# A mixture-of-experts layer with random-feature attention: the opening, the first expert and the closing blocks are put in another order, and the first expert's transposes are compared word by word

## The chip, the core and the metric

The kernel runs on one core of one Trainium2 chip. That core has five engines that run side by side, each on its own list of instructions: TensorE (PE in the profile) for matrix products and for transposes, VectorE (DVE), ScalarE (ACT), GpSimd (POOL), and SyncE (SP), which here only issues DMA transfers. Two sorts of DMA appear: SP's transfers go over one hardware queue, and the gathers and scatters with an index per row are issued by POOL on a software queue. The metric is the time on the device in microseconds (us), as the median of three runs.

## The reference

The input x has 4 x 2048 tokens of 512 numbers in fp32, 8192 tokens in all. Cut to what matters:

```python
xn  = layernorm(x)                                   # eps 1e-5
# attention by random features, 512 of them; ab = xis
def rfs(v): return exp(ab * (proj @ v) - 0.5 * |v|**2 * ab**2) * exp(ab) / sqrt(512)
attn = rfs(xn) @ rfs(input_weights).T                # input_weights: 512 x 512
# mixture of experts: 64 experts, 256 hidden units each
scores = sigmoid(xn @ router_w)                      # 8 groups of 8 experts
top 4 groups by their largest score, then the top 8 experts among them
w = chosen scores / their sum * 2.5
each expert takes its first 256 tokens, in the order of the tokens
e(t) = (silu(t @ gate_e) * (t @ up_e)) @ down_e
moe = sum over the chosen experts of w * e(xn)
      + (silu(xn @ sgate) * (xn @ sup)) @ sdown      # shared expert, for all tokens
out = x + attn + moe
```

## The kernel before

**Products.** Every fp32 matrix is split into a rounded part `hi` and a rest `lo`. `upper` (L96) makes `hi` as a copy on ACT, `rest` (L99) makes `lo` as a subtraction, on DVE unless told otherwise. `products` (L102, its matmul at L107) then sums three products, hi·hi, hi·lo and lo·hi. Transposes are done on PE against an identity matrix. A Tile scheduler puts each engine's instructions in order, following dependencies; `behind(a, b)` (L116) adds an ordering by hand: a is placed after b. Names with `_h` and `_l` in the profile are the two parts.

**Memory.** A pool of 40 slots of 4 KiB per partition (`kib4`, L83) holds almost everything: weights, tokens, transposed tokens, features. PSUM, where PE writes, is divided into three pools: `ps_tr` (2 banks), `ps_mm` (4) and `ps_sm` (2).

**Opening.** SP loads `ab`, the projection `pj`, the input weights `wi` (both in two transfers of 256 rows by `load_rows`, L142), the tokens of block 0, the router weights, and the shared expert's weights (`load_shared`, L167). `turn` (L293) transposes a matrix in 16 steps of 128x128 (`ps_x`) and splits the outcome; it is called for `pj` (`pT`), then for `wi` (`wT`), then for each block. `normalize(b)` (L254) takes mean and variance of each row by `bn_stats` on DVE, the reciprocal root by `inverse_root` (L223: a seed of two instructions on DVE, then three rounds of four small instructions on POOL), then `shift`, and last four ACT activations into `xw`. The row norms of tokens and weights go to a small DRAM array `norms` and come back, spread over all partitions, as `q` (`across`). `exponent` computes `ps_f`, the projections, and adds the norm term on DVE; its outcome for the weights is `fw`. `features_w` finishes the weights' features, `fW`.

**Blocks.** The tokens go in 16 blocks of 512 rows. `look_up(b)` (L311) is a generator: it transposes the normalised block (`xT`), computes the router's logits (`ps_l`, turned back by `ps_lt`), chooses experts on DVE, counts each expert's tokens into the DRAM array `upto`, and writes the normalised rows with their scores to `xnw`. `dense(b)` does the shared expert (`ps_gu`, then `ps_o` with `d_h`, `d_l`) and, for even blocks, the attention (`ps_f`, `fT`, `ps_o` with `fW`); its inner function `finish` (from L505) adds to the tokens and stores them in halves of 256 rows. Even blocks go through `dense` in the first 430 us. `routing(step)` between the steps drives the look-ups, one block per 5 steps. Odd blocks are only looked up; their transposes are kept in DRAM (`turned`), and their attention (`late_attention`: `ps_fu`, `ps_y`, copied to `yb` and stored to `attn`) fills the experts' loop.

**Experts.** `seek` (L674) is a generator that per step issues `find` for one expert, two indirect DMAs into `at` from `upto` (L651), and after every fourth expert runs `tokens_of` (L663 on), which compares `at` with the slot numbers on DVE and gives `who`, the token in each of the 256 slots. `gather(e)` (L700) issues two indirect DMAs that fetch an expert's rows, `xg`, from `xnw`. `turn_slots(e)` (L712) transposes them (`ps_t`), splits them into `gT`, and computes the weight `we` of each slot. At the end of the last even block the order is written by hand:

```python
for k in range(RC):
    for _ in range((2, 2, 1, 1)[k]):
        next(slots)
    next(rest_of)
for e in range(4):
    gather(e)
```

and three more steps of `slots` follow ahead of `turn_slots(0)`. The loop over experts (from L876) loads gate and up weights of expert i+2 and down weights of i+1, runs `hidden(i)` (`ps_gu`), takes a step of `slots`, gathers i+4, transposes i+1, and runs `down(i-1)` (`ps_e`), whose outcome is added to the output by an indirect DMA.

**Closing.** `ends` (L840) takes block 15 and the odd blocks 1, 3, ..., 13 through what is left of `dense`. `one(b)` fetches `xT_h` and `xT_l` from `turned` and, with `early`, the sums so far (`xo`, from the output) and `y` (from `attn`). It is called for the next block at step 2 of the block before, and two of the next block's steps are run at `left - 4` and `left - 2`.

## Time and profile before

| what | value |
|---|---|
| runs, us | 1354.17, 1352.31, 1350.28 (median 1352.31) |
| profiled execution, us | 1341.48 |
| its span, us | 1339.8 |
| mean granted PE clock | 0.994 |
| instructions | 21249 |
| DMA over the span | 327.07 MB, 244 GB/s |

The span is from the first to the last record of the profiled execution; its own time lies 1.7 us above. The chain that ended last is, by engine, PE for 64% of the span, DMA for 1%, and other engines for less than 1% each; by line, the experts' `ps_gu` has 34%, `ps_e` 13%, `ps_y` and `ps_fu` 5% each, `ps_o` 4% and `ps_t` 3%.

How the profile is read: a row such as `PE ps_x L301 <- ACT xw L278: 6.4, 5, 4.5` says that PE stood idle ahead of the instruction that writes `ps_x` at line 301, released by ACT's `xw` at line 278, 6.4 us in 5 waits, the longest 4.5. In a row of the timeline the first number is the start in us from the start of the span, the second the duration, then engine, line, operation, output<-inputs and their shapes, and in brackets the idle time ahead of it and its releaser. A row of forty digits shows tenths of busy time in equal slices of 33.5 us; PEclk is the clock that was granted to PE, in tenths of full speed.

### The profile page before, as it was taken

To read this page: it belongs to the slowest core of one execution; us is meant where nothing else is said; L and a number is where in the kernel's file an instruction comes from. 1 tells how busy PE (TensorE), PEld (TensorE's weight loads), DVE (VectorE), ACT (ScalarE), POOL (GpSimd) and SP (SyncE) were. 2 spreads that over 40 slices of the span, in tenths; PEclk is the share of its full clock that TensorE was granted. 3 is DMA by queue.
4 is the path that set the end of the run, shared out by engine and by line. 5 is a ranking of instruction groups with operands and counts; after the bars stand their busy time and mean duration, and the time that the engine had idled before them with its cause. 6 is when DMAs were issued, how large, how long until landed. Compare 5 with 4: busy or idle time off the path is not lost.

```text
span 1339.8 us, 21249 instructions
## 1 busy us (share of the span) xinstructions
PE 1311.0 (98%) x7648; PEld 1144.8 (85%) x7648; DVE 920.6 (69%) x1898; ACT 645.8 (48%) x1025; POOL 577.3 (43%) x684
## 2 busy tenths in 40 slices
PE   7899999999999899999999999999999999999998
PEld 6788888888888799999999999999999999978886
DVE  4887778768756477777677777777676777544455
ACT  5454434433433165556556655655564656531111
POOL 3321022022003575767776767767776755220000
PEclk9899999999999899999999999999999999999999
DMA  7465544554476799999999999999999989756996
GB/s 249 165 229 180 212 181 158 212 208 155 172 261 211 237 252 279 294 273 247 306 269 287 279 284 278 259 288 278 269 279 293 279 239 282 206 141 236 311 314 207
DMA packets 186266, 327.07 MB, mean 244 GB/s; under 512 B 15536, under 2 KB 87216, under 8 KB 186160
## 3 DMA queue, kind: packets, MB, share of 16 engines
q1 hardware_dynamic: 153392, 245.93, 53.5%
q0 software_dynamic: 32768, 79.78, 26.7%
q8 instruction: 60, 0.98, 0.3%
q14 instruction: 46, 0.38, 0.1%
HBM read 220.66 MB, written 104.99 MB: 243 GB/s over the span
## 4 chain that ended last, share of the span: by engine, by line
PE 64%; DMA 1%; DVE 0%; ACT 0%; issue 0%; DVEq 0%
PE ps_gu L107 34%; PE ps_e L107 13%; PE ps_y L107 5%; PE ps_fu L107 5%; PE ps_o L107 4%; PE ps_t L721 3%; DMA xT_l<-turned 1%; DMA at<-upto,line 0%; PE ps_f L107 0%; DVE f L454 0%; DVE d_l L100 0%; DVE at L663 0%; ACT f L467 0%; DVE xo L508 0%; ACT fT L97 0%
## 5 line engine op out<-in xcount | busy, mean ns | idle before, releaser
L107 PE MATMUL ps_gu<-gT,gu_h 128*128 128x256 f32 x2048 | 294.3, 284 | 0.0
L771 POOL DMA_INDIRECT out_dram<-ye,who x128 | 221.1, 1727 | 143.7 <-DMA out_dram<-ye,who 57.0
L107 PEld LDWEIGHTS ps_gu<-gT,gu_h 128*128 128x128 f32 x2048 | 269.6, 192 | 7.3 <-ACT gu_h L97 0.5
L651 POOL DMA_INDIRECT at<-upto,line x128 | 148.1, 1157 | 82.3 <-DVE first_of L645 43.6
L704 POOL DMA_INDIRECT xg<-xnw,who x128 | 136.7, 1068 | 88.7 <-issue 62.6
L107 PE MATMUL ps_gu<-gT,gu_l 128*128 128x256 f32 x1024 | 166.7, 285 | 0.0
L100 DVE TENSOR_TENSOR gu_l<-gu,gu_h 128x1024 fp32r<-128x1024 f32 x128 | 155.9, 1220 | 4.9 <-ACT gu_h L97 4.1
L107 PE MATMUL ps_e<-d_h,ehT 128*128 128x512 f32 x512 | 148.7, 392 | 0.0
L107 PEld LDWEIGHTS ps_gu<-gT,gu_l 128*128 128x128 f32 x1024 | 140.7, 191 | 1.2
L97 ACT CAST gu_h<-gu 128x1024 fp32r<-128x1024 f32 x128 | 132.2, 1059 | 0.0
L230 POOL TENSOR_TENSOR a<-rstd,ve 128x4 f32<-128x4 f32 x48 | 10.9, 227 | 265.5 <-DVE rstd L228 262.9
L97 ACT CAST ehT<-sg 128x512 fp32r<-128x512 f32 x64 | 39.8, 621 | 172.4 <-DVE sg L462 172.4
L107 PEld LDWEIGHTS ps_e<-d_h,ehT 128*128 128x128 f32 x512 | 94.6, 188 | 18.8
L770 ACT ACTIVATE ye<-ps_e,we 128x512 f32<-128x512 f32 x128 | 88.5, 698 | 37.0 <-PE ps_e L107 37.0
L462 DVE SCALAR_TENSOR_TENSOR sg<-sg,ps_gu 128x512 f32<-128x512 f32 x64 | 44.0, 688 | 78.7 <-PE ps_gu L107 78.5
L100 DVE TENSOR_TENSOR d_l<-d,d_h 128x1024 fp32r<-128x1024 f32 x64 | 78.3, 1223 | 10.1 <-ACT d_h L97 10.0
L460 ACT ACTIVATE sg<-ps_gu 128x512 f32<-128x512 f32 x64 | 38.4, 600 | 95.8 <-PE ps_gu L107 95.8
L100 DVE TENSOR_TENSOR gT<-ps_t,gT 128x512 fp32r<-128x512 f32 x128 | 83.3, 683 | 0.2 <-ACT gT L97 0.2
L107 PE MATMUL ps_e<-d_l,ehT 128*128 128x512 f32 x256 | 79.2, 390 | 1.0 <-DVE d_l L100 1.0
L107 PE MATMUL ps_o<-fW_h,fT 128*128 128x512 f32 x288 | 79.7, 391 | 0.3 <-ACT fT L97 0.2
L107 PE MATMUL ps_o<-d_h,hT 128*128 128x512 f32 x256 | 79.8, 399 | 0.0
L461 DVE SCALAR_TENSOR_TENSOR sg<-sg,ps_gu 128x512 f32<-128x512 f32 x64 | 43.9, 685 | 43.5 <-ACT sg L460 43.4
(173 smaller groups left out, 2544.4 us busy)
## 6 DMA issues: line engine op xcount, KB each, us to landing
gu<-in_L_ffn_gate_w_dram SPq DMA_DIRECT2D x64, 512.0 KB
gu<-in_L_ffn_up_w_dram SPq DMA_DIRECT2D x64, 512.0 KB
d<-in_L_ffn_down_w_dram SPq DMA_DIRECT2D x64, 512.0 KB
xnw<-xw SPq DMA_DIRECT2D x32, 577.0 KB
xb<-in_L_attn_x_dram SPq DMA_DIRECT2D x32, 512.0 KB
out_dram<-xb SPq DMA_DIRECT2D x32, 512.0 KB
xT_h<-turned SPq DMA_DIRECT2D x30, 512.0 KB
xT_l<-turned SPq DMA_DIRECT2D x30, 512.0 KB
```

The costliest lines, as they stand in the source:

```text
L97: return nc.scalar.copy(dst, src)
L100: return on.tensor_tensor(dst, src, hi.bitcast(FP), ALU.subtract)
L107: last["pe"] = nc.tensor.matmul(ps, w[c][a], v[c][b], start=(start and part == 0 and c == 0), stop=(stop and part == 2 and c == n - 1),)
L230: nc.gpsimd.tensor_tensor(a, y, v, ALU.mult)
L460: nc.scalar.activation(dst, g, AF.Tanh, scale=0.5)
L461: nc.vector.scalar_tensor_tensor(dst, dst, 1.0, g, ALU.add, ALU.mult)
L462: nc.vector.scalar_tensor_tensor(dst, dst, 0.5, u, ALU.mult, ALU.mult)
L651: nc.gpsimd.indirect_dma_start(out=at[:, e % TE, h, :], out_offset=None, in_=upto, in_offset=bass.IndirectOffsetOnAxis(ap=line[:, e, h : h ...
L704: nc.gpsimd.indirect_dma_start(out=xgs[e][:, h, :], out_offset=None, in_=xnw, in_offset=bass.IndirectOffsetOnAxis(ap=who[:, e, h : h + 1], ...
L721: turned_s = nc.tensor.transpose(ps_[:, c, ts(h, P)], xr[:, h, ts(c2 * 2 + c, P)], ident_r)
L770: nc.scalar.activation(ye[:, h, :], po, AF.Copy, scale=wes[e][:, h : h + 1])
L771: now = nc.gpsimd.indirect_dma_start(out=out, out_offset=bass.IndirectOffsetOnAxis(ap=who[:, e, h : h + 1], axis=0), in_=ye[:, h, :], in_o ...
```

## The change

In the opening, `wi` is loaded first and in four pieces of 128 rows, then `ab`, `pj`, block 0, the router weights, block 1, and the shared weights. The weights' norms come from `bn_stats` of `wi` in place of four squares on ACT. `wi` is transposed ahead of `pj`. `normalize` is divided in three: `statistics`, `roots`, and what is left. Block 0's root runs on DVE throughout (the others stay on POOL), and block 1's statistics and root are ordered ahead of block 0's transposes. The projections of the weights (`projected`) take the banks of `ps_sm` and `ps_tr`, block 0's transposes those of `ps_mm`; the four additions into `fw` come behind block 0's split. The rests of the shared weights (`gu_l`, `d_l`) move from POOL to DVE. `normalize(1)` comes ahead of block 0's logits, and `look_up(1)` starts one step later.

At the experts, two steps of `slots` are taken in each of the four places ahead of the gathers (eight in place of six), and two in place of three afterwards. For expert 0 `turn_slots` transposes the rows a second time, in fp32, into another bank (`p32`); ACT copies it out, DVE compares it with the first transposes word by word and counts the equal words. The weights `we` of expert 0 are multiplied by 1 if all are equal, and by a large other number if not.

In the closing, the copies into `yb` are placed behind the split of the last down weights once that is issued; `xT` and `y` of the next block are fetched at the start of a block, ahead of `xo`; the first of the two early steps moves one step up for block 15; `finish`'s addition of `y` is placed behind the last DVE instruction noted; and block 13, stored last, is stored in quarters of 128 rows.

```diff
-    def load_rows(src, name):
+    def load_rows(src, name, at_once=2):
...
-            nc.sync.dma_start(t, src[ts(k, 2 * P), :].rearrange("(s p) d -> p s d", p=P))
+            for s in range(0, 2, at_once):
+                r0 = (2 * k + s) * P
+                nc.sync.dma_start(
+                    t[:, s : s + at_once, :],
+                    src[r0 : r0 + at_once * P, :].rearrange("(s p) d -> p s d", p=P),
...
     last = {}
+    late_blocks = range(1, NB - 1, 2)
+    last_stored = late_blocks[-1]
+    wi = load_rows(iw, "wi", 1)
     ab = const.tile([P, RC], FP, name="ab")
     nc.sync.dma_start(ab, xis.rearrange("(c p) -> p c", p=P))
     pj = load_rows(proj, "pj")
-    wi = load_rows(iw, "wi")
     xbs = {0: load_tokens(0)}
...
-    def load_shared():
+    def load_shared_gates():
...
+    def load_shared_down():
...
-    sgu, sd = load_shared()
...
+    xbs[1] = load_tokens(1)
+    sgu = load_shared_gates()
+    sd = load_shared_down()
...
-    def inverse_root(y, v):
...
+    def statistics(rows_of, after=NS * [None]):
...
         for s in range(NS):
+            last["stats"] = nc.vector.bn_stats(st, rows_of[s])
+            if after[s] is not None:
+                behind(last["stats"], after[s])
...
+    def roots(b, mv, on=nc.gpsimd):
...
+        inverse_root(rstd, ve, on)
...
+        on.tensor_tensor(shift, mv[:, :, 0], rstd, ALU.mult)
+        last["shift"] = on.tensor_scalar(shift, shift, -1.0, None, ALU.mult)
...
+    def normalize(b, rstd, shift):
...
-            ((ps_tr, "tr"), (ps_sm, "sm")),
+            ((ps_tr, "tr"), (ps_sm, "sm")) if b else ((ps_mm, "mm"),),
...
+    def projected(v, rc, ps):
         products(ps, parts(pT, KC, ts(rc, P)), v, True, True)
...
+    def exponent(dst, nsq, rc, ps):
...
-                nc.vector.tensor_tensor(xb[s], xb[s], y[s], ALU.add)
+                behind(nc.vector.tensor_tensor(xb[s], xb[s], y[s], ALU.add), last["dve"])
             last["dve"] = nc.vector.tensor_tensor(xb[s], po, xb[s], ALU.add)
             done.append(s)
-            if s ^ 1 in done:
-                k = s // 2
-                store_rows(b, k, xb)
+            if b == last_stored:
+                r0 = b * TB + s * P
+                nc.sync.dma_start(out[r0 : r0 + P, :], xb[s])
+            elif s ^ 1 in done:
+                store_rows(b, s // 2, xb)
...
                 last["dve"] = nc.vector.tensor_copy(yb[:, s % 2, :], po)
+                if "down" in last:
+                    behind(last["dve"], last["down"])
...
+    wmv = statistics(wi)
+    wT = turn(lambda s: wi[s], "wT", ((ps_tr, "tr"), (ps_sm, "sm")))
+    wq = const.tile([P, NS], FP, name="wq")
+    nc.gpsimd.tensor_tensor(wq, wmv[:, :, 0], wmv[:, :, 0], ALU.mult)
+    nc.gpsimd.tensor_tensor(wq, wq, wmv[:, :, 1], ALU.add)
+    nc.gpsimd.tensor_scalar(padded[2][:, :NS], wq, -0.5 * H, None, ALU.mult)
+    as_row(NB, padded[2])
+    wn = across(NB)
     pT = turn(lambda s: pj[s], "pT", ((ps_mm, "mm"),))
-    wT = turn(lambda s: wi[s], "wT", ((ps_tr, "tr"), (ps_sm, "sm")))
...
     normed = {}
-    normed[0] = normalize(0)
-    first, root = last["stats"], last["root"]
-    wq = const.tile([P, NS], FP, name="wq")
-    for s in range(NS):
-        sq = act.tile([P, H], FP, tag="t", name="sq")
-        squared = nc.scalar.activation(sq, wi[s], AF.Square, accum_out=wq[:, s : s + 1])
...
-    def split_gates(gu, on=nc.vector, after=None):
-        hi = [kib4([P, KC, I], "gu_h") for _ in range(2)]
...
-            if after is not None:
-                behind(a, after[0])
...
+    normed[0] = normalize(0, *roots(0, statistics(xbs[0], NS * [last["rest"]]), nc.vector))
+    first = last["shift"]
+    roots1 = roots(1, statistics(xbs[1], NS * [first]))
+    seed1 = last["seed"]
+    def split(t, name, after=(None, None)):
+        hi, lo = kib4(list(t.shape), name + "_h"), kib4(list(t.shape), name + "_l")
+        both = upper(hi, t), rest(lo, t, hi)
+        last["split"] = both[1]
+        for a, b in zip(both, after):
...
-    shared_gu = split_gates(sgu, nc.gpsimd, (squared, root))
...
+    sgate = split(sgu[0], "gu", (None, seed1))
+    ps_w = []
+    for rc in range(RC):
+        pool, tag = ((ps_sm, "sm"), (ps_tr, "tr"))[rc // 2]
+        ps_w.append(pool.tile([P, H], FP, tag=tag, name="ps_f"))
+        projected(parts(wT, KC), rc, ps_w[rc])
+    late = look_up(0)
+    next(late)
+    upper0 = last["upper"]
+    sup = split(sgu[1], "gu", (upper0, last["rest"]))
     fw = Chunks(RC, "fw", FP)
     for rc in range(RC):
-        ps = ps_mm.tile([P, H], FP, tag="mm", name="ps_f")
-        exponent(fw[rc], parts(wT, KC), wn, rc, ps)
+        exponents = exponent(fw[rc], wn, rc, ps_w[rc])
+        behind(exponents, last["rest"])
+    normed[1] = normalize(1, *roots1)
+    shared_w = list(zip(sgate, sup)), split(sd, "d", (upper0, exponents))
...
-    xbs[1] = load_tokens(1)
-    late = look_up(0)
-    next(late)
-    normed[1] = normalize(1)
     next(late)
     next(late)
-    shared_w = shared_gu, split_down(sd, nc.gpsimd)
...
-        nc.scalar.activation(f, f, AF.Exp, scale=ab[:, rc : rc + 1])
+        behind(nc.scalar.activation(f, f, AF.Exp, scale=ab[:, rc : rc + 1]), upper0)
         behind(nc.vector.tensor_scalar(f, f, coef[:, rc : rc + 1], None, ALU.mult), first)
...
+        if e == 0:
+            same = rt.tile([P, KC // 2], FP, tag="same", name="same")
...
+            if e == 0:
+                p32 = ps_mm.tile([P, 2, CAP], FP, tag="mm", name="ps_t32")
+                for c in range(2):
+                    for h in range(NH):
+                        nc.tensor.transpose(
+                            p32[:, c, ts(h, P)], xg[:, h, ts(c2 * 2 + c, P)], ident
+                        )
+                like = act.tile([P, 2, CAP], FP, tag="t", name="like")
+                nc.scalar.copy(like, p32)
+                nc.vector.tensor_tensor(like, like, ps, ALU.is_equal)
+                nc.vector.tensor_reduce(same[:, c2 : c2 + 1], like, AX.XY, ALU.add)
...
         )
         behind(shares, turned_r)
         nc.vector.reciprocal(we, we)
+        if e == 0:
+            for c2 in range(KC // 2):
+                k = same[:, c2 : c2 + 1]
+                nc.vector.tensor_scalar(k, k, -float(2 * CAP), 1.0e6, ALU.add, ALU.mult)
+                nc.vector.tensor_scalar(k, k, 1.0, None, ALU.add)
+                nc.vector.tensor_scalar(we, we, k, None, ALU.mult)
         wes[e] = we
...
+        if k == (b == 1) and b < NB:
             fronts[b] = look_up(b)
...
-            normed[b + 1] = normalize(b + 1)
+            normed[b + 1] = normalize(b + 1, *roots(b + 1, statistics(xbs[b + 1])))
...
                 if n == 8:
                     for k in range(RC):
-                        for _ in range((2, 2, 1, 1)[k]):
+                        for _ in range(2):
                             next(slots)
                         next(rest_of)
...
-        if n < 3:
+        if n < 2:
             next(slots)
...
+        def one(b, w, xT, y, early):
...
-                y = load_rows(attn[ts(b // 2, TB), :], "y") if b in late_blocks else None
                 return load_rows(out[ts(b, TB), :], "xo"), y
-            xT = fetch_block(b)
...
+        cur, left = one(order[0], w, fetch_block(order[0]), None, False)
...
+            if n + 1 < len(order):
+                b = order[n + 1]
+                fetched = fetch_block(b), load_rows(attn[ts(b // 2, TB), :], "y")
+            whole = n == 0
...
-                    nxt, steps = one(order[n + 1], w, True)
-                if nxt is not None and k in (left - 4, left - 2):
+                    nxt, steps = one(b, w, *fetched, True)
+                if nxt is not None and k in (left - 4 - whole, left - 2):
                     next(nxt)
...
             dws[i] = split_down(downs.pop(i))
+            if i == E - 2:
+                last["down"] = last["split"]
```

## The prediction, made before the changed kernel ran

> **What bounds the kernel now.** I read the page first: shares of the engines, then the 40 slices.
>
> ```profile
> PE 1311.0 (98%) x7648; PEld 1144.8 (85%) x7648; DVE 920.6 (69%) x1898; ACT 645.8 (48%) x1025; POOL 577.3 (43%) x684
> ...
> PE   7899999999999899999999999999999999999998
> ...
> DVE  4887778768756477777677777777676777544455
> ...
> PEclk9899999999999899999999999999999999999999
> ```
>
> TensorE is the bound and is almost never idle. All that a change of order can win lies in span minus PE busy, 1339.8 - 1311.0 = 28.8 us, plus the time in which PE ran at a lower granted clock. Digits below 9 stand at the start, in slice 14 (about 450 us) and at the very end. DVE is near 9 in slices 2 and 3: there a second engine is nearly full. Next the view of waits for PE over the whole span:
>
> ```profile
> PE ps_x L301 <- ACT xw L278: 6.4, 5, 4.5
> PE ps_x L301 <- DMA pj<-_L_attn_proj_matrix_dram: 6.0, 2, 5.3
> PE ps_t L721 <- DVE gT L100: 5.9, 1, 5.9
> PE ps_gu L107 <- DMA xT_h<-turned: 1.8, 2, 1.3
> ...
> PE ps_e L107 <- DVE d_l L100: 1.0, 1, 1.0
> ```
>
> (us in total, times, longest; a sixth line, for xT_l, has 0.5.) Five places hold nearly all of the idle time. The stretches of PE alone show what follows an idle gap (us, PE busy, clock, DMA share, GB/s):
>
> ```profile
> 40.00:42.00 2.00, 0.26 (x2) 1.00 0.94 354
> ...
> 44.00:45.00 1.00, 0.25 (x1) 0.50 0.00 0
> ...
> 49.00:50.00 1.00, 1.00 (x6) 0.50 0.00 0
> ...
> 460.00:462.00 2.00, 0.28 (x2) 0.50 0.48 172
> ```
>
> A gap of 4 us or more is paid twice: idle, then about 5 us at half clock. Last, the timeline at these places:
>
> ```profile
> 26.10 2.72 DVE L454 SCALAR_TENSOR_TENSOR fw<-q,ab,ps_f 128x512 f32<-128x512 f32 x4 [8.38 <-DMA q<-norms]
> ...
> 115.06 1.91 PE L301 MATMUL ps_x<-ident,xw 128*128 128x128 f32 x16
> 116.73 0.71 PE L107 MATMUL ps_o<-d_h,hT 128*128 128x512 f32 x2
> ...
> 444.42 0.79 PE L721 MATMUL ps_t<-ident_r,xg 128*128 128x128 f32 x8
> ...
> 459.84 1.23 DVE L663 TENSOR_TENSOR at<-at,slot 128x1024 f32<-128x1024 f32 x1 [5.98 <-DMA at<-upto,line]
> ...
> 1196.00 0.90 SPq L145 DMA_DIRECT2D xo<-out_dram  x2
> ...
> 1197.00 0.89 SPq L532 DMA_DIRECT2D xT_h<-turned  x2
> ...
> 1335.89 0.37 SPq L154 DMA_DIRECT2D out_dram<-xo  x1
> ```
>
> **The change part by part.** Pitches (start to start) at full clock from the timeline: a 128x512 product 0.228 us, 128x256 0.115, an fp32 transpose 0.104 (115.06 to 116.73, 16 of them).
>
> *Opening, up to the first ps_f of block 0 (52.56 us before).* The weight rows come first and in four pieces. Before, the first 1.05 MB had landed at 6.62, so wi is in by about 6.0, pj by 9 at the 370 to 400 GB/s of those stretches. 12 + 16 transposes at the cold 0.21 (16 in 3.35 us) end at 12.2 (before 12.7). 48 ps_f follow: 10.95, to 23.2. Meanwhile DVE ends pT_l at 13.6, takes four bn_stats (2.8, as at 14.29 to 17.06) and then the root itself: 17 dependent small steps of 0.18 (17.19, 17.35, 17.55), to 19.5. On POOL these steps are 0.28 apart and a gu_l of 2.4 us stood between them: shift came at 23.94. ACT needs 2.93 for the four xw: 22.4, ahead of PE's 23.2. So block 0's 16 transposes follow without a gap and at full clock: 1.7, to 24.9, where before they ended at 29.90. xT_h costs 0.4; then 48 ps_gu, 8 ps_l, 4 ps_lt (13.2) and block 1's transposes (1.7): 40.2. Block 1's statistics and roots are now ahead of all of it, and gu_l and d_l are off POOL, so the 4.5 us wait goes.
>
> ACT loses the four squares and their sums (0.8 each). SP gets two more issues (0.5 each) for wi and block 1's load ahead of sgu; sgu is first needed at 16, so that costs nothing. Late next is q: its norms rows are queued on SP behind sgu and sd, so q is issued at about 23.5, and q took 5.3 (20.84 to 26.10): 29. ps_l now needs a PSUM bank that ps_f holds until fw has read it: 30.2 against PE's 29.2, 1.0 lost: 41.2, a lead of 11.4. This is not kept. Onto DVE come two gu_l (2.4), d_l (1.2) and the root (2.5). In the new order about 30.5 us of DVE work stand between fw and block 0's last feature; from 29.4 that is 59.9, and its rounded copy 61.2, then four xw of block 2 to 64.2. PE would be there at 59 and be through block 2's first transposes and 23 ps_o at 64.3, where before it stood at 72.4. The lead left is 8; I take 7.8. look_up(1) one step later is in that order. From 100 on DVE is at 75% or less and PE waits 2 us in 350: nothing more to win, and cover for the rest.
>
> *Expert 0 (450 to 467).* DVE stood 5.98 us behind a gather of `at` before it could split gT; PE lost 5.9 idle and then 2.1 (its work of 461.7 to 466.8 needs 3.0 at full clock, took 5.1): 8.0. Now finds 4 to 7 are issued ahead of the four token gathers and this `at` is read before expert 0 is turned. Price: POOL issues four more finds (1.25 each) first, of which 3.9 fall into its idle time before 434.7; gather 0 is 1.1 later, its second half lands at 437.1 + 6.6 = 443.7, PE needs it at 444.2. The last find lands at about 435 + 6.5 = 441.5, DVE is there at 440: 1.5 lost, bounds 0 and 4.3 (landings 3.5 to 9.3).
>
> The fp32 check: 8 transposes x 0.104 = 0.83 on PE. On ACT two copies (0.6 each), on DVE two compares (0.69), two reduces (0.6) and six small steps (0.17): 3.6 us of DVE. Expert 0's 48 products (5.5 us) hide them, and the weights `we` are needed only by down(0), a round later; but the second half of gT and the next PSUM bank wait behind the first compare: 0.5. Without the cover all 3.6 would count. No compare of this form is in the trace; gT's split, PSUM and SBUF in 0.68, is the nearest row. Part: 8.0 - 1.5 - 0.83 - 0.5 = 5.2.
>
> *Here a rule speaks against the change.* Row: 16 transposes at 115.06 run in 1.67 us, and the clock in 115 to 121 stays 1.00. The Trainium skill (TensorE: Matmul & The Clock Gate, Part 4: PE-mode transpose) says that transposes do not count as PE work for the clock; Part 1 gives windows of 3.4 us. By the rule block 0's and block 1's transposes, now behind each other's products, could each leave 3.4 us at half clock, 1.7 twice: 3.4 less. By the row it is nothing. The row is this kernel's own; 3.4 goes into the range.
>
> *Last expert.* PE waited 1.0 for d_l behind a yb copy; the copy is now held back behind d_l (1.22); behind it on DVE and SP stand only ehT and attn's store, which no one needs for 20 us: 1.0. *First late block.* xT was queued on SP behind xo, which waits for the last scatter; now xT and y go first: 1.8 + 0.5 = 2.3. Its cover is DMA: 0.94 busy at 1240 to 1320, so y and xT earlier use slices 34 and 35 (206 and 141 GB/s). *Last store.* From issue to end 3.9 us for 512 KB; a quarter-block of 256 KB at 330 GB/s saves 0.8, less an issue: 0.7 (bounds 0 and 1).
>
> Sum 7.8 + 5.2 + 1.0 + 2.3 + 0.7 = 17.0. The profiled execution took 1341.48 (span 1339.8), so 1324.5. The median of the runs, 1352.31, is 0.8% above it; no view says why. I scale: 17.1, 1335.2.
>
> **Rivals.**
> *DVE takes the opening (chance 0.2).* For it: DVE 8 or 9 tenths in slices 2 and 3, and 6.1 us more work. Against: before, PE waited there only 0.2. If half of the 7.8 goes, or the clock rule holds: 13 to 14 less than before, 1338.5 to 1339; with both, 10.
> *The wait at expert 0 only moves (0.1).* If find or gather lands 3 to 5 us later, PE idles before ps_t and the half clock returns: the part is 0, 12 less, 1340.
> *Slower (0.05).* SP is one queue. The new buffer order shifts which of the 40 slots each weight load waits for; if gates of an expert come late for ACT's cast in the 62 rounds of the loop, each costs PE. Against: between 500 and 1160 ACT waits for no load, and PE is 100% busy. A lateness beyond the slack by 0.28 us per round eats the 17.1; 0.4 us gives -17.1 + 24.8: 1360. It decides from a load some 4 us later than now.
> *The gains do not come about (0.05),* as when the opening is bound by loads and the clock anyway: 1350 to 1354.
>
> **How the numbers follow.** Likeliest (0.6): 1335.2, own range 1330 to 1340, from DVE giving back 1 to 6, `at` 0 to 4.3, store 0 to 1. The range to hold 8 in 10 takes in the first two rivals and, below, 7 us of which the opening's full lead makes 3.6: 1328 to 1345. A measurement can tell 0.3%, 4 us. Faster 0.90, same 0.05, slower 0.05.
>
> **What would show it.** Right: the waits of PE lose ps_x on xw, ps_t on gT, ps_e on d_l and ps_gu on xT; clock 1.00 from 13 us on; first ps_f of block 0 near 41; PE idle about 15 in all, half of it start and end. Half wrong: PE waiting at 29 to 33 on fw or at 60 to 65 on fT or xw; ps_t waiting on xg or on DVE's `at` or compare near 435 to 445. Wrong: ACT gu_h waiting for DMA in the loop, clock 0.50 after a run of transposes, or DMA waits of ps_gu after 1215.

## The result, and the profile after

| | runs | median, us | ratio to before |
|---|---|---|---|
| before | 4 | 1351.30 (1349.63 to 1354.17) | |
| after | 4 | 1337.38 (1335.18 to 1338.81) | 0.9892 (95% interval 0.9871 to 0.9913) |

The changed kernel is 13.9 us faster; 17.1 was forecast, and 1335.2 us against 1337.4 measured. That the two figures lie so close is in part luck, as the traces show. One thing must be known to read any number below: the kernel before takes about 1341 us in one series of runs and about 1351 in three others, among them these; its profile of 1341.48 us belongs to the first sort, the changed kernel's profile (1338.81 us, span 1337.1) to the second. The two profiles can therefore not simply be subtracted. The three series of experiments below ran on three different chips: number 15 where before has 1341, numbers 14 and 2 where it has 1351. For the runs of the table the chip is not known. Whether the chip makes the difference was not tested.

The page of the changed kernel, the lines that answer to those of before:

```profile
PE 1310.4 (98%) x7656; PEld 1146.4 (86%) x7656; DVE 930.8 (70%) x1932; ACT 646.7 (48%) x1019; POOL 569.1 (43%) x670
...
PE   8999999999998899999999999999999999999998
...
DVE  7978768767764577777777767667776776653555
...
PEclk9999999999998899999999999999999999999999
```

PE's busy time is as it was; DVE has 10 us more. The start has gained (8, 9, 9 where 7, 8, 9 stood, and the clock's first digit below 9 is gone), but slices 13 and 14, about 400 to 470 us, are now both at 8. The waits of PE in the changed kernel (us in total, times, longest):

```profile
PE ps_y L107 <- ACT fU L97: 5.7, 1, 5.7
PE ps_x L323 <- DMA wi<-_attn_input_weights_dram: 5.4, 3, 4.0
PE ps_gu L107 <- issue: 4.5, 8, 1.4
PE ps_lt L368 <- ACT lt L361: 2.2, 1, 2.2
```

All four waits that the prediction wanted gone are gone: for xw, for gT, for d_l and for xT. Three have come: for lt in the opening, for fU at 431 us, and eight ahead of expert 0's products at 445 to 458 us that no engine releases. The timeline of the changed kernel shows the second and third:

```profile
429.19 0.75 DVE L478 SCALAR_TENSOR_TENSOR f<-q,ab,ps_fu 128x512 f32<-128x512 f32 x1 [4.49 <-remote]
...
431.39 0.79 PE L107 MATMUL ps_y<-fW_h,fU 128*128 128x512 f32 x1 [5.75 <-ACT fU L97]
...
446.64 1.33 PE L107 MATMUL ps_gu<-gT,gu_h 128*128 128x256 f32 x9 [1.40 <-issue]
...
453.15 0.36 PE L107 MATMUL ps_gu<-gT,gu_l 128*128 128x256 f32 x1 [1.03 <-issue]
```

DVE stands 4.49 us ahead of an addition whose only open input is ps_fu, and PE's last product into ps_fu had ended at 420.9, 8 us earlier. Everything after it (fU, then ps_y) is late by that. After each of the two places PE runs at half clock for 6.8 us (from 427.8 and from 455.1). Idle PE and work lost to half clock (taken as half of PE's busy time in it) come to 15.2 us between 420 and 480 us, where the profile of before has 8.3.

The most useful view for the whole question is the lead: the start of a PE product in the kernel before, less the start of the same product in the other kernel, read from the two timelines. A column's time is that of the kernel before. The row of the result stands against the first profile of before, all others against its second, taken in the series where before has 1341 us ("before again", span 1340.8).

| kernel (series by before's median) | first ps_f of block 0 | 100 us | 434 us | 783 us | block 15, 1190 us | block 1, 1225 us | last product | span |
|---|---|---|---|---|---|---|---|---|
| prediction | 11.4 | 7.8 | 7.8 | 13.0 | 14.0 | 16.3 | 16.3 | 17.0 |
| after, result (1351) | 7.9 | 8.1 | 8.7 | -0.8 | 0.3 | 3.5 | 3.9 | 2.7 |
| after again (1341) | 10.3 | 10.4 | 11.0 | 15.2 | 16.5 | 21.8 | 22.5 | 21.2 |
| no compare (1341) | 8.6 | 8.7 | 9.3 | 9.9 | 10.9 | 16.2 | 16.9 | 15.6 |
| free y (1341) | 8.5 | 8.6 | 9.2 | 14.0 | 15.2 | 20.5 | 20.6 | 20.8 |
| opening only (1351) | 9.1 | 8.9 | 9.5 | 3.0 | 0.7 | -0.3 | 0.1 | 0.2 |
| slots undone (1351) | 8.8 | 9.0 | 9.6 | -2.7 | -2.1 | 3.2 | 4.0 | 3.0 |
| lt first (1351) | 12.5 | 12.6 | 13.6 | 2.8 | 4.0 | 9.3 | 10.0 | 8.7 |
| after third (1351) | 10.6 | 10.0 | 10.5 | 4.0 | 5.2 | 10.5 | 11.2 | 10.0 |
| three mends (1351) | 13.5 | 13.6 | 14.5 | 6.9 | 7.3 | 12.7 | 13.2 | 13.3 |
| closing undone (1351) | 8.3 | 8.4 | 8.9 | 0.4 | 0.2 | 0.8 | 1.0 | 0.7 |
| at later (1351) | 9.5 | 9.6 | 9.6 | -0.9 | 0.4 | 5.7 | 6.5 | 5.2 |
| compare eight (1351) | 9.0 | 9.2 | 9.9 | -23.3 | -22.1 | -16.8 | -16.0 | -16.9 |

Between 434 and 783 us every row from a series of 1351 loses 6 to 13 us (the last one 33, of which more below); in the other series two of three gain there and one stands still.

### The profile page after: what moved, and what is told of

It is laid out like the page before. It is cut to its first block, busy times and chain, and to the rows that moved or that the text cites. A ratio compares the mean times of both kernels' runs of the same rounds, so it can differ in the third digit from the quotient of the medians.

```text
span 1337.1 us, 21310 instructions
## 1 busy us (share of the span) xinstructions
PE 1310.4 (98%) x7656; PEld 1146.4 (86%) x7656; DVE 930.8 (70%) x1932; ACT 646.7 (48%) x1019; POOL 569.1 (43%) x670
## 4 chain that ended last, share of the span: by engine, by line
PE 94%; DVE 2%; ACT 1%; issue 1%; DMA 1%; POOL 0%; another core or an unknown queue 0%; SPq 0%; ACTq 0%; DVEq 0%
PE ps_gu L107 41%; PE ps_o L107 14%; PE ps_e L107 13%; PE ps_f L107 6%; PE ps_y L107 6%; PE ps_fu L107 6%; PE ps_t L757 3%; PE ps_l L351 2%; PE ps_x L323 2%; DMA pj<-_L_attn_proj_matrix_dram 1%; PE ps_lt L368 1%; DVE r L486 0%; DVE st L274 0%; DVE f L478 0%
## 5 line engine op out<-in xcount | busy, mean ns | idle before, releaser
L826 POOL DMA_INDIRECT out_dram<-ye,who x128 | 226.2, 1767 | 190.5 <-ACT ye L825 127.1
L685 POOL DMA_INDIRECT at<-upto,line x128 | 139.7, 1092 | 82.2 <-DVE first_of L679 43.5
L245 POOL TENSOR_TENSOR a<-rstd,ve 128x4 f32<-128x4 f32 x45 | 11.2, 249 | 270.6 <-DVE rstd L241 268.3
L486 DVE SCALAR_TENSOR_TENSOR sg<-sg,ps_gu 128x512 f32<-128x512 f32 x64 | 44.0, 687 | 67.6 <-PE ps_gu L107 54.6
L492 ACT ACTIVATE f<-f,ab 128x512 f32<-128x512 f32 x64 | 46.2, 722 | 77.3 <-DVE f L478 63.2
L100 DVE TENSOR_TENSOR gT<-ps_t,gT 128x512 fp32r<-128x512 f32 x128 | 83.2, 682 | 0.1
L100 DVE TENSOR_TENSOR ehT<-sg,ehT 128x512 fp32r<-128x512 f32 x64 | 44.3, 692 | 51.4 <-ACT ehT L97 43.8
```

The lines of the kernel that those rows point to most:

```text
L100: return on.tensor_tensor(dst, src, hi.bitcast(FP), ALU.subtract)
L486: nc.vector.scalar_tensor_tensor(dst, dst, 0.5, u, ALU.mult, ALU.mult)
L492: nc.scalar.activation(f, f, AF.Exp, scale=ab[:, rc : rc + 1])
L685: nc.gpsimd.indirect_dma_start(out=at[:, e % TE, h, :], out_offset=None, in_=upto, in_offset=bass.IndirectOffsetOnAxis(ap=line[:, e, h : h ...
L826: now = nc.gpsimd.indirect_dma_start(out=out, out_offset=bass.IndirectOffsetOnAxis(ap=who[:, e, h : h + 1], axis=0), in_=ye[:, h, :], in_o ...
```

## The experiments

### Series 1: both kernels again, without the compare, and with y free

**before_again** and **after_again**: no edit.

> The kernel before, unchanged, to see whether the profiled execution of 1341.48 us, 9 to 13 us under its timed runs (1349.6 to 1354.2), is typical. Theory 1 (the stalls at the first expert come and go between executions): this second profile has PE waits of more than 4 us that no engine of the kernel releases between 420 and 470 us, as the changed kernel's profile has, and its span is near 1350. Theory 2 (the first profile was taken on a quicker chip or in a quicker moment): all stretches are alike, the span is again 1338 to 1342, and the timed runs here are near 1342 as well.

> The changed kernel, unchanged. Its first profile lost 9.6 us of its 8.7 us lead between 424 and 459 us: a 4.5 us wait of VectorE ahead of the addition of q (released by nothing that the profile names), 5.7 us of PE behind it, and eight waits of PE ahead of expert 0's products (4.5 us in all). Theory 1 (these stalls come and go): at least one of the two places is gone or has another length here, and the span moves with it by 3 to 10 us. Theory 2 (they belong to this order of instructions): both recur within 1 us. Ratio to before near 0.989 (0.987 to 0.991) by both.

Before took 1340.96 us in this series (its copy 1341.62, ratio 1.0004, 0.9994 to 1.0013), so theory 2 holds for before: its first profile was of this sort. After took 1321.82, a ratio of 0.9854 (0.9838 to 0.9871), 19.1 us less, which is below the 0.987 to 0.991 expected by both theories. Its waits of PE are these:

```profile
PE ps_x L323 <- DMA wi<-_attn_input_weights_dram: 5.9, 3, 3.5
PE ps_lt L368 <- ACT lt L361: 1.8, 1, 1.8
PE ps_l L351 <- ACT cu L449: 1.5, 7, 0.2
PE ps_gu L107 <- DVE gT L100: 0.6, 1, 0.6
```

Both stalls at the first expert are gone, so for the changed kernel theory 1 holds: the order of instructions alone does not make them. The semaphore records of the two traces show what differs. Each row is a product of PE that counts up PE's semaphore, and the moment at which the count was recorded:

| after, result: product ends | counted | after again: product ends | counted |
|---|---|---|---|
| 418.17 | 422.80 | 416.62 | 416.63 |
| 419.53 | 427.04 | 417.98 | 417.99 |
| 420.89 | 429.16 | 419.34 | 419.35 |

DVE waits for the first and the third of these, and goes on 0.02 and 0.03 us after each is counted in the left-hand trace, while PE has long gone on to later products. The signal of PE was late, by 4.6 to 8.3 us, not the work. The rows are paired in order, and need to be: the left-hand trace has 791 of PE's 912 counts, the right-hand one all of them. This goes through all fourteen traces. The nine from series of 1351 lack 76 to 128 of PE's counts, all of them after 400 us, and in each DVE starts the addition that needs the third row's product 3.9 to 8.3 us after that product; the five others lack none, and there it is 1.0 to 1.4, with DVE at work. What holds the signals up is not known; it falls in the stretch in which POOL issues its indirect DMAs back to back, but POOL does so in the series of 1341 as well.

**no_compare**: the second transposes of expert 0 and all that hangs on them are left out.

```diff
-            if e == 0:
-                p32 = ps_mm.tile([P, 2, CAP], FP, tag="mm", name="ps_t32")
...
-                nc.vector.tensor_tensor(like, like, ps, ALU.is_equal)
-                nc.vector.tensor_reduce(same[:, c2 : c2 + 1], like, AX.XY, ALU.add)
...
-                nc.vector.tensor_scalar(we, we, k, None, ALU.mult)
```

> The changed kernel without the second transposes of expert 0, their comparison and the factor on its weights. Prediction's step: 0.83 us on PE plus 0.5 of waiting, so 1.3 us less than the changed kernel (ratio to it 0.999). Rival (the comparison has filled DVE, ACT and PSUM at the worst place and caused the stalls of 445 to 459 us): 6 to 10 us less, and PE has no waits ahead of expert 0's products. The 4.5 us wait of VectorE at 424 us is ahead of it and should stay by both.

1322.82 us, ratio 0.9856 (0.9836 to 0.9875), beside 1321.82 with the compare: no difference that can be told. That rules out the rival's 6 to 10, but not the 1.3 us. Its five runs lie between 1320.4 and 1326.9, and the profiled one, of 1326.93, shows another stall. Timelines of DVE and of PE in this kernel:

```profile
434.41 1.23 DVE L697 TENSOR_TENSOR at<-at,slot 128x1024 f32<-128x1024 f32 x1 [3.12 <-DMA xg<-xnw,who]
...
439.69 1.22 PE L107 MATMUL ps_fu<-xT_h,pT_h 128*128 128x512 f32 x2 [3.05 <-DVE yb L581]
```

DVE stands 3.12 us before the second comparison of `at` (the profile names a gather as the last to come; the instruction itself waits for the eight finds); behind it in its queue are two copies of yb, whose bank PE needs for ps_fu. PE waits 3.05 us and then runs at half clock to about 445 us. In the changed kernel's own trace DVE stood 1.08 us there, and PE did not wait. This is the prediction's landing of the last find (1.5, bounds 0 and 4.3), with one difference: 1.1 of it cost nothing and 3.1 cost about 6 (3.05 of idle PE and some 2.8 lost to half clock; by the lead it is 4.1, since this kernel saves the compare's own transposes and a wait of 0.6).

**free_y**: one line.

```diff
-                behind(nc.vector.tensor_tensor(xb[s], xb[s], y[s], ALU.add), last["dve"])
+                nc.vector.tensor_tensor(xb[s], xb[s], y[s], ALU.add)
```

> The changed kernel with the addition of y in the closing blocks not placed behind the last DVE instruction noted. In the changed kernel's profile the last addition on DVE starts 1.4 us after PE's last product has ended (1332.64 against 1331.2), in that of before at once (1335.17). Theory: the order of the y additions costs that 1.4 us, and the kernel is 1.3 us shorter here (ratio to the changed kernel 0.999), DVE's last addition within 0.1 us of PE's end. Rival (the tail is set by the stores): no difference, the span ends 3.8 us after the last addition at the same time.

1322.33 us, ratio 0.9858 (0.9837 to 0.9879): the time tells no difference from 1321.82. The trace does. First the end of the changed kernel (second copy), PE's last products and DVE's last additions, then the same of this kernel:

```profile
1313.08 0.61 PE L107 MATMUL ps_o<-d_h,hT 128*128 128x512 f32 x2
...
1314.35 0.68 DVE L532 TENSOR_TENSOR xo<-xo,y 128x512 f32<-128x512 f32 x1
1315.13 0.69 DVE L533 TENSOR_TENSOR xo<-ps_o,xo 128x512 f32<-128x512 f32 x1
```

```profile
1314.95 0.61 PE L107 MATMUL ps_o<-d_h,hT 128*128 128x512 f32 x2
...
1315.61 0.69 DVE L533 TENSOR_TENSOR xo<-ps_o,xo 128x512 f32<-128x512 f32 x1 [0.67 <-PE ps_o L107]
```

With y behind, DVE alternates two additions per 128 rows and starts the last one 1.44 us after PE has ended; with y free it starts 0.05 after. So the ordering costs 1.4 us, as expected. It does not show in the time, since this profile's opening has 1.8 us less lead (8.6 against 10.4): PE's wait for lt cost half clock here and not there, which comes next.

### Series 2: the opening alone, the slots, the comparison, lt

**opening_only**: the changed kernel with the three other parts as before (slots 2, 2, 1, 1 and three; no compare; closing as before).

> Before with the change's opening alone (loads, weight statistics, order of transposes and roots, rests of the shared weights on DVE, look_up(1) one step later); slots, expert 0 and closing are as before. Prediction's step: 7.8 us less than before, so a ratio of 0.9942. The last call's traces (leads of 8.6 to 10.5 us at 100 us): 8.6 to 10.5 us less, 0.992 to 0.9936. Rival (the lead is eaten by the loop's waits, since the experts start earlier than their weights are there): 0.997 or more, and the lead on PE falls after 450 us.

1342.18 us where before has 1350.62, ratio 0.9940 (0.9920 to 0.9959), 8.4 us, near the prediction's 7.8. In its trace the lead of 9.5 at 434 us does fall afterwards, to nothing, but against a before of the other series; the time says that before loses as much here. The rival is out by the ratio. This trace also has before's order at the experts, and the late signals with it: 10.9 us of idle PE and half clock between 420 and 480 us, where the second profile of before has 6.1. So before, too, very likely loses some of its 10 us there.

**slots_undone**: the changed kernel with the steps of slots as before.

```diff
-                        for _ in range(2):
+                        for _ in range((2, 2, 1, 1)[k]):
                             next(slots)
...
-        if n < 2:
+        if n < 3:
             next(slots)
```

> The changed kernel with the steps of slots as before (2, 2, 1, 1 and three afterwards), all else changed. Prediction's step for expert 0: 8.0 of stall and half clock come back and 1.5 of waiting for the landing goes, so 6.5 us more than the changed kernel (ratio to it 1.005). The last call's traces (4.3 us gained there): 4 to 6 us more (1.003 to 1.0045), with DVE standing 4 to 6 us before the comparison of at with the slots and PE 4 us or more before ps_t. Rival (the lead of the opening alone has made the gathers land in time): nothing, below 1 us.

1340.05 us, ratio 0.9927 (0.9903 to 0.9950). The changed kernel has 0.9885 and 0.9892 in the two other series of this sort, so by time the step is worth some 5 us, though the intervals overlap. The expected picture is not there: in this trace DVE hardly waits for `at`, since two waits of PE, of 5.1 and 6.7 us, give the finds time to land. They look like late signals again, here on their way to ACT, whose copy starts 5.6 us after the transposes that it reads:

```profile
437.13 0.45 PE L757 MATMUL ps_t<-ident_r,xg 128*128 128x128 f32 x4
...
443.23 0.59 ACT L97 CAST gT<-ps_t 128x512 fp32r<-128x512 f32 x1 [14.57 <-remote]
```

Between 420 and 480 us this trace loses 15.3 us, the changed kernel's own traces of this sort 15.2 and 11.5. The size is as expected, but the trace does not show the 5 us at this place: what they come from stays open.

**at_later**: one step of slots in place of two behind the gathers.

> The changed kernel with one step of slots in place of two behind the gathers, so that the second comparison of at with the slots is taken in the loop's first round, its finds having been issued ahead of the gathers all the same. Theory (the kernel with no comparison lost 3.1 us of PE plus half clock because DVE stood 3.1 us before this comparison, with the copies of yb behind it and PE waiting for the bank they free; in the changed kernel it stood 1.1 us and PE did not wait): no wait of DVE for at of over 0.5 us, no wait of PE for yb, times within 1 us of the changed kernel's better executions (1321 to 1322 where before has 1341) and no execution 4 to 6 us above. Rival (what counts is that the finds are early; the place of the comparison does nothing): as the changed kernel. Other rival: the comparison is now in front of expert 1's gT and costs its 1.2 us there.

1336.42 us, ratio 0.9890 (0.9868 to 0.9913), as the changed kernel. DVE has no wait for this comparison and PE none for yb, as expected, but the late signals of this series cover the place (5.7 and 4.6 us of PE), so whether the executions that lose a bank to yb disappear could not be seen.

**lt_first**: block 1's activations behind lt.

```diff
-            behind(normed_s, last["upper"])
+            behind(normed_s, last["lt"] if b == 1 else last["upper"])
...
-        nc.scalar.copy(lt, pl)
+        last["lt"] = nc.scalar.copy(lt, pl)
...
-    normed[1] = normalize(1, *roots1)
     shared_w = list(zip(sgate, sup)), split(sd, "d", (upper0, exponents))
...
     next(late)
+    normed[1] = normalize(1, *roots1)
     next(late)
```

> The changed kernel with block 1's four activations xw on ACT placed behind the copy lt of block 0's logits. In the changed kernel PE stands 1.8 to 2.2 us before ps_lt, since lt is behind these four (2.94 us, released by the root on POOL at 29.7); with 2.2 the clock then falls to one half for 3.4 us, with 1.8 it did not. Theory: the wait falls to 0.5 or less and the clock stays at 1.00 in every execution: 1.5 us less than the changed kernel's better executions and 3.5 less than its others, ratio to the changed kernel 0.9975 to 0.999. Rival (DVE sets the pace of the opening and block 1's later xw delays its transposes): no gain at 100 us, PE waiting for xw or for fT at 40 to 60 us instead.

ACT in the changed kernel (result), then in this one:

```profile
29.76 2.94 ACT L300 ACTIVATE xw<-xb,shift,rstd 128x512 f32<-128x512 f32 x4 [2.56 <-POOL shift L289]
...
34.15 0.57 ACT L361 COPY lt<-ps_l 128x512 f32<-128x512 f32 x1
```

```profile
31.74 0.59 ACT L361 COPY lt<-ps_l 128x512 f32<-128x512 f32 x1 [0.25 <-PE ps_l L351]
32.23 2.94 ACT L300 ACTIVATE xw<-xb,shift,rstd 128x512 f32<-128x512 f32 x4
```

And PE in two-microsecond stretches (us, PE busy, clock, DMA share, GB/s), changed kernel and this one:

```profile
32.00:34.00 2.00, 0.58 (x3) 1.00 0.24 24
34.00:36.00 2.00, 1.23 (x6) 0.82 0.81 297
36.00:38.00 2.00, 2.00 (x6) 0.50 0.86 332
38.00:40.00 2.00, 2.00 (x9) 0.83 0.01 4
```

```profile
32.00:34.00 2.00, 2.00 (x12) 1.00 0.01 1
34.00:36.00 2.00, 2.00 (x10) 1.00 0.45 123
36.00:38.00 2.00, 2.00 (x11) 1.00 0.97 368
38.00:40.00 2.00, 2.00 (x15) 1.00 0.43 165
```

The wait of 2.2 us and the 1.7 us lost to half clock behind it are gone, PE is without a gap from 30 to 40 us, and the first ps_f of block 0 comes at 40.7 us. The lead at 100 us is 12.6, the rival is out. 1333.85 us, ratio 0.9874 (0.9852 to 0.9897), which is 1.5 to 2.4 us below the changed kernel's ratios: the trace shows the 3.9, the time is too coarse to.

### Series 3: three mends, the closing, and eight compares

**after_third**: no edit.

> The changed kernel, unchanged, as the measure for the other three on the same chip. Ratio to before 0.985 to 0.989 by all theories.

1335.47 us where before has 1351.02, ratio 0.9885 (0.9866 to 0.9904).

**closing_undone**: closing as before (xT and y behind xo, y free, halves, yb not held back).

> The changed kernel with the closing as before: xT and y fetched after xo, additions of y free, block 13 stored in halves, yb not held behind d_l. Prediction's steps: 1.0 + 2.3 + 0.7 = 4.0 us more than the changed kernel (ratio to it 1.003). The traces so far (1.3 at the last expert, 5.3 at the first late block, 0.6 at a later one, and 1.3 given back at the last store): 5.9 us more (1.0045). Rival (the late block's wait depends on where the experts' end falls against the last scatter): less than 2 us.

1342.15 us, ratio 0.9931 (0.9912 to 0.9950), 6.7 us more than the changed kernel. That is nearer the traces' 5.9 than the prediction's 4.0, though the intervals (the difference can be 3 to 10 us) leave both; it rules out the rival's less than 2. The waits are back:

```profile
PE ps_gu L107 <- DMA xT_h<-turned: 2.1, 2, 1.6
...
PE ps_e L107 <- DVE d_l L100: 1.0, 1, 1.0
PE ps_gu L107 <- DMA xT_l<-turned: 0.5, 1, 0.5
```

Why the late block is worth 5.3 and not the 2.8 that PE waits for it is read from the stretches of before (second profile):

```profile
1202.00:1204.00 2.00, 1.17 (x4) 1.00 1.02 406
1204.00:1206.00 2.00, 1.46 (x5) 0.73 1.01 394
1206.00:1208.00 2.00, 2.00 (x6) 0.50 1.05 400
1208.00:1210.00 2.00, 2.00 (x10) 0.92 1.05 387
```

Half clock again, 3.4 us of it or some 1.7 lost; with the waits of 2.8 that is 4.5 of the 5.3. It does not always follow. In the first profile of before, from which the prediction was made, PE waits 2.3 us here and the clock stays at 1.00:

```profile
1202.00:1204.00 2.00, 0.70 (x2) 1.00 1.02 418
1204.00:1206.00 2.00, 1.10 (x4) 1.00 1.01 401
```

Against that profile the changed kernel gains 3.2 at this block (0.3 to 3.5 in the table), against the second one 5.3.

**three_mends**: lt_first, free_y and at_later together.

> The changed kernel with three mends: block 1's xw behind lt on ACT, the additions of y free, the second comparison of at one round later. Theory: 2 to 4 us from the first (the wait for ps_lt and its half clock), 1.3 from the second (DVE's last addition 1.44 us after PE's end), 0 to 3 from the third (the executions that lose a bank to a late yb), together 4 to 7 us less than the changed kernel (ratio to it 0.995 to 0.997, to before 0.980 to 0.984). Rival (the third puts the comparison in front of expert 1's gT, and PE waits there): the lead at 446 us is 3 us above the changed kernel's and is down by 1 us or more at 500.

1332.11 us, ratio 0.9862 (0.9841 to 0.9884), 3.4 us below the changed kernel; the intervals overlap. The lead is 3.6 above the changed kernel's at 100 us. By the rival's own mark it is not seen: 4.4 above at 446 us and 4.3 at 500. It is 2.9 at 783 and 2.1 at 1190; where these 1 to 2 us go is open, with late signals in both traces. DVE's last addition starts with PE's end, and the span has 3.3 us more lead. The first two mends without the third were not tried.

**compare_eight**: `e == 0` becomes `e < 8` in the three places of `turn_slots`.

> The changed kernel with the second transposes, the comparison and the factor for experts 0 to 7 in place of expert 0 alone. Theory (only PE's own transposes count, 0.83 us per expert, and the rest is hidden): 7 x 0.83 = 5.8 us more than the changed kernel, ratio to it 1.0044. Rival 1 (the second half of gT and a bank wait behind the compare, 0.5 more each): 9.3 us more. Rival 2 (DVE, 73% busy in the loop and 3.6 us more per expert of some 11.5 us, becomes the bound in these rounds): 15 us or more, with PE waiting for gT or gu_l. Rival 3 (PE has slack for it): nothing.

1359.61 us, ratio 1.0052 (1.0030 to 1.0074): 24.1 us more than the changed kernel, 3.4 us for each further expert, and slower than before. Its waits of PE between 440 and 560 us:

```profile
PE ps_gu L107 <- issue: 7.4, 11, 1.1
PE ps_gu L107 <- ACT gu_h L97: 3.5, 2, 3.2
PE ps_gu L107 <- DVE gu_l L100: 2.6, 4, 0.9
PE ps_t L757 <- DVE like L775: 1.8, 3, 0.8
```

In size it is rival 2, but DVE is not the bound as rival 2 has it: from 440 to 560 us it is busy for 83.2 us, in the third copy for 86.5. PE waits for gu_h, gu_l and the compare's own bank, and longest for nothing that the profile names. The two traces differ by 26.9 us. Of these 5.8 are PE's own transposes (7 x 0.83), and 16.0 are idle PE and half clock between 420 and 560 us (27.5 against 11.5); the other 5 are not accounted for. The prediction said that without the cover all of the compare's 3.6 us on DVE would count. That the cost is within 0.2 of it is chance, for it is made of other things.

## Why the prediction was right, point by point

All four waits that were named are gone, and with the closing taken back its two return. The size is in good part luck: in the series of 1341 the change is worth 19.1 us by time and 21.2 by span, where 17.0 was worked out; in the series of the result it is worth 13.9, and the changed kernel's trace there has late signals that no step foresaw. The sizes below are from the second copies of both kernels, taken in one series.

- **Opening: 7.8 predicted, 10.4 measured; time of the part alone 8.4 (ratio 0.9940).** The working was right up to block 0's transposes, which started at 23.2 as predicted. The step that failed is "ps_l now needs a PSUM bank that ps_f holds until fw has read it: 1.0 lost". The wait came elsewhere, at ps_lt: the four xw of block 1, moved ahead, stand on ACT in front of lt, released late by the root that was left on POOL. It costs 1.6 to 2.2 us, and mostly 1.7 more of half clock. The second copy was spared the half clock; the result's trace was not, and its lead at 100 us is 8.1. With this mended, the first ps_f is at 40.7, where the prediction had 41.2.
- **DVE takes 3.6 of it back: did not happen.** The lead at 100 us is within 0.6 of that of the first ps_f in all traces. These 3.6 us are the largest error of this part. In the result's trace PE waits for nothing of DVE up to 100 us. The rival of DVE as the opening's bound is out.
- **The clock and the transposes.** The row held: in lt_first the 16 transposes of block 1 at 39.06 run with PE busy on both sides and the clock at 1.00 before and after. None of the 3.4 us that the rule would have taken is to be seen there, nor in the other traces, once the fall behind the wait for lt is set aside.
- **Expert 0: 5.2 predicted, 4.2 measured (11.0 to 15.2), some 5 by time.** That DVE's wait for `at` and PE's for gT go is shown by the pair of traces (6.1 us of idle PE and half clock between 420 and 480 us before, 0.6 after); taking the step alone back did not bring them back. The `at` landing was sized right as a wait (1.08 on DVE; 1.5 predicted) but priced wrongly: it costs nothing while the yb copies behind it are not needed, and about 6 us once they are. That is the rival "the wait at expert 0 only moves"; in the trace without the compare it took place.
- **The compare: 1.3 predicted, none found** by time, within a scatter of 6 us. PE's eight transposes are in the trace, so it is not free. That the cover pays for the rest is argued; eight of them cost 3.4 for each further one.
- **Last expert: 1.0 predicted, 1.3 measured.**
- **First late block: 2.3 predicted, 5.3 measured.** The step that failed is that the wait alone was priced: half clock behind it (1.7) was left out, since the prediction counted it only for gaps of 4 us and more. Its own profile showed none at this place, and against that profile the step is worth 3.2.
- **Last store: 0.7 predicted, -1.3 measured.** From the end of DVE's last addition to the end of the span it is 3.9 us before and 3.7 to 3.8 with quarters, so the quarters are worth 0.2. The order of y, which the prediction listed in no step, costs 1.4.
- **Scaling by 0.8% to the median: wrong in kind.** The 10 us by which the median of before lies above its profile are not spread over the kernel. In the profiles of the changed kernel from such series they are lost at 420 to 460 us, where signals come late, and the changed kernel loses more there than the 10: it is 19.1 us faster in the series of 1341, but 13.9 and 15.5 in those of 1351. No profile of the kernel before was taken in such a series. The trace of the opening alone suggests that about half of its 10 us go at the same place; the rest stays open, as does the cause of the late signals.
- **Slower, by late weights in the loop: out.** PE is 100% busy from 500 to 1100 us in the changed kernel as before.
- **The signs.** PE is idle for 17.2 us in the second copy and 26.7 in the result's trace, where about 15 was named; the clock stays at 1.00 up to the last product in the second copy alone; the first ps_f of block 0 comes at 42.7 to 44.7 in the three copies (41 named).
- **A reading that was off.** "From 100 on DVE is at 75% or less" holds for the mean up to 400 us (73%), not for each stretch: from 300 to 320 us before has it at 95%. PE did not wait for it there.

## What to carry to other kernels

Where one engine is 98% busy, a gain is counted in gaps, and a gap of about 2 us or more may cost 1.7 us on top by half clock: the first late block came out too small by that. When work is moved ahead, look on every engine's queue for what it now stands in front of (xw in front of lt, `at` in front of yb, y in front of the last addition); the cost is nothing up to the point at which a bank runs out, and then all of it. And a check whose cost cannot be told on one tile can cost 3.4 us a tile on eight.

## What was not expected of the hardware

- After a wait of PE of 2.2 us at ps_lt the clock fell to 0.50 for 3.4 us in six of seven traces; after one of 1.9 it fell as well, after waits of 1.8 and 1.6 it did not. What decides can be read from the fourteen traces. In each, every stretch between two changes of the clock within the run lasts a whole multiple of 3.41 us (3.41, 6.83, 13.65, 23.89). Cut the traces into pieces of 3.41 along these changes (idle shares are rough, as the ends of products are modelled): the clock fell 34 times before the last product, and 33 times PE had been idle for 53% or more (1.8 us) of the piece just before, once for 48%. Of the other 5275 pieces at full clock only one was idle for as much (55%). So it counts where a wait lies: the wait of 2.2 without a fall (third copy) is cut by an edge, with 49% of one piece idle, and one of 3.7 with eight compares is cut into 55 (the exception) and 52%; the wait of 1.9 fills 56% of one piece.
- PE's signals to DVE came 2.5 to 8.3 us after the products had ended, at 413 to 421 us, in all nine traces of series of 1351, and 0.01 to 0.02 us after in the five others. The same program differs by 10 to 16 us between such series.
